# A planner that weaves convolutions into a stream of absolute differences: TensorE's rates, its slack and the place of ScalarE's sums changed in its account

## The chip, the cores and the metric

The kernel runs on one core of a Trainium2 chip. A core has TensorE (PE) for matrix products, VectorE (DVE) and ScalarE (ACT) for element work, GpSimd (POOL), SyncE (SP) for most DMA issues, and 16 DMA engines. The metric is the device time of one execution in microseconds (us), as the median of several executions.

## The reference

The input x has 16 images of 32 channels of 128 x 128. Four layers are applied, each as x = x + f(gn(x)), with gn a normalisation over groups of two channels:

```python
x = x + _L0_conv_ref(_gn(x), ...)   # skewed rows through an LSTM-like recurrence over the width
x = x + _L1_conv_ref(_gn(x), ...)   # AdderNet: out = -sum |patch - w| over 32 channels x 9 taps, on quantised values
x = x + _L2_conv_ref(_gn(x), ...)   # 2-d Hartley transform, mix 32 x 32 modes, transform back
x = x + _L3_conv_ref(_gn(x), ...)   # five edge operators, each normalised; conv, pool, conv, pool, conv, pool,
                                    # conv, and three (deconv, conv) pairs; times the input
```

Layer 1 is the long one here: for each of 32 output channels, 288 values of |patch - w| are summed at every place of every image. No matrix product does this. The kernel makes max(patch - w, 0) for whole tiles on DVE or ACT and lets TensorE add them up over the channels.

## The kernel before, in words

**Stage 0** (to about 685 us of the trace) does the first layer. The change doesn't touch it.

**The differences** (class `Differences`, method `run`, L682 on) do the second layer in 32 halves: 16 images with two halves of 64 rows each. A half has 72 steps (8 groups of four output channels by 9 taps). Each step makes one difference tile of 128 partitions by 64 rows by 128 columns, on DVE (L760, three buffers) or on ACT (L757, two buffers), whichever would end first by the account. For each difference TensorE issues a *sum*: 16 products (L647) into four PSUM banks. Nine *linear* taps a half (L662) add the part of |a - b| that is linear in a. At the end of a half DVE takes the result out of PSUM (`finish`, L628) and stores it. Four images form a group, and when a group's images are done, the third and fourth layers can run for it.

**The background** (class `After`) does the third and fourth layer for groups 0, 1 and 2 beside the differences, and for group 3 after them. It is a Python generator. Each `yield us` hands over the TensorE time of the products just issued; `yield -us` asks for a pause; `yield SUMMED` asks to wait until TensorE is done by the account. Its parts, in order, for each group:

- forward transform (L1110, L1125, L1082), mixing of modes in 32 ky steps (L1221), whose weights come in eight loads of 1024 KB through three buffers
- inverse transform: 32 steps into `o1` (L1295), then 16 steps back to full size with the residual (L1345)
- Gram products for the statistics of the edge operators (L1487), 128 steps
- the folded operators and conv1: side columns in 22 steps (L1837), then eight chunks of 16 rows with 25 taps each (L1863), each chunk followed by edge additions (L1898), pooling (L1757) and ACT's spread into `y1` (L1771)
- conv2 to conv4 (L1661), the composed upsampling layers (L908, L934), and the last one, in four units of two rounds with two sets of four taps, which DVE multiplies into the residual (L2024)

**The planner** (class `Weave`) decides while the program is written in which order each engine gets its instructions; nothing is decided on the chip. It keeps three accounts, `pe`, `dve` and `act`, which say when each engine will be done. After each difference on DVE, `run` issues the sums of all differences that have ended by DVE's account (local function `sums`), and charges PE_US for each. Then `advance(due)` runs background steps as long as TensorE could start one early enough before `due`, the time at which the next sum will be asked for:

```python
            start = max(self.pe, self.ready)
            if start + 1.0 > due + SLACK:
                return
            us = self.step()
            if us:
                self.pe = start + us * CLOCK
```

If TensorE is still early after that, `keep_busy` issues products with zeros (L677). Evictions that follow `SUMMED` are put into DVE's order at `lag()` after the present, which is the account's lateness of TensorE plus 1.0. `keep_order` then fixes each engine's order as it was written, so an instruction that waits holds up everything behind it on its engine.

**The drain** (`drain`): once the differences are written, what is left of group 2 and all of group 3 are written alternately, the one whose own clock is earlier first; `SUMMED` is then a fixed 4.5, pauses are stretched by 1.5 while both live, and mixing makes no pauses.

Of the kernel before, what the change touches and what calls it, by code (L numbers as in the profile page):

```python
# [485 lines left out]

DVE_US, ACT_US, PE_US = 2.36, 7.15, 1.0
LATE = 1.5
SLACK, CLOCK = 3.0, 1.0
SUMMED = ("summed",)  # L490
# [29 lines left out]
class Differences:  # L520
# [134 lines left out]
    def linear(self, acc, q, tap):  # L655

        kh, kw = tap // 3, tap % 3
        for j in range(4):
            for k in range(4):
                rows = slice(32 * k, 32 * k + 32)  # L660
                row = 16 * j + 4 * k + kh
                self.nc.tensor.matmul(  # L662
                    acc[k][32 * j : 32 * j + 32, :],
                    self.sel16[rows, 8, :],
                    q[rows, row : row + 4, kw : kw + W],
                    start=False,
                    stop=False,
                )
        self.weave.pe = max(self.weave.pe, self.weave.now) + 0.45

    def keep_busy(self, acc, q, until):


        start = max(self.weave.pe, self.weave.now)
        for k in range(min(int((until - start - 0.1) / 0.25), 4)):
            for j in range(4):
                self.nc.tensor.matmul(  # L677
                    acc[k][32 * j : 32 * j + 32, :], self.zero, q[:, :4, :W], start=False, stop=False
                )
            self.weave.pe = start + 0.25 * (k + 1)  # L680

    def run(self, tc, ctx, weave):  # L682
# [29 lines left out]
        for b in range(B):  # L712
            for half in range(2):
                q, xq = following, xq if half else {}
                unit = {"b": b, "half": half, "acc": None, "late": [], "summed": 0}
                for i in range(72):
# [36 lines left out]
                    dst = t if kw == 1 else t[:, :, :W]  # L753
                    unit["late"].append((ends[act], i, act, t))
                    count[act] += 1
# [77 lines left out]
class Composed:  # L833
# [60 lines left out]
    def round(self, src, n, acc, pick, quarter=0):  # L894
# [5 lines left out]
        nc, t = self.nc, self.t  # L900
        for tap in range(4):
            for j in range(4):
                for blk in range(4):
# [11 lines left out]
                    )  # L915
            yield rows * n / 512 * 0.2 + 0.95
            if tap != 2:
# [45 lines left out]
class After:  # L963
# [76 lines left out]
    def forward(self, g):  # L1040
# [4 lines left out]
        with self.pool("t_m") as mp:  # L1045
# [6 lines left out]
            with self.pool("t_t") as tp, ExitStack() as rows:  # L1052
# [24 lines left out]
                def second(n):  # L1077
# [21 lines left out]
                    steps[n] = outs[n] = weave.summed(out)  # L1099
                    return 1.45  # L1100

# [4 lines left out]
                def first(n):  # L1106
# [10 lines left out]
                    ready[n, 0] = weave.summed(out)  # L1117
                    return 1.05

                def turned(n):  # L1120

                    weave.done(ready[n, 0])
                    p = self.acc()
                    for a in range(4):
                        nc.tensor.transpose(p[:, 128 * a : 128 * a + 128], ta[n][:, a, :], cst["ident128"])  # L1125
                    ready[n, 1] = weave.summed(lambda: scaled(n, p))
                    return 1.5

# [82 lines left out]
    def mixing(self, g, xs, wp, wt):  # L1211
# [5 lines left out]
        for ky in range(M1):  # L1217
# [10 lines left out]
            if ky % 4 == 3 and len(wt) < M1 // 4:  # L1228
                wt.append(self.weights(wp, len(wt)))
            yield 1.0  # L1230
            if ky % 4 == 3 and 8 < ky < M1 - 1 and not weave.draining:
                yield -2.5
        yield SUMMED
# [14 lines left out]
    def back(self, g, load):  # L1248
# [6 lines left out]
        with self.pool("t_z") as zp_, self.pool("t_r", ahead) as rp:  # L1255
# [33 lines left out]
            for oh in range(2):  # L1289
                pa = [self.acc() for _ in range(4)]  # L1290
                for o in range(16):
                    for r in range(4):
                        for blk in range(4):
# [7 lines left out]
                            )  # L1301
                    yield 1.1
                yield SUMMED
# [35 lines left out]
            for n in range(16):  # L1339
                s, half = n // 2, n % 2  # L1340
                pf = [self.acc() for _ in range(2)]
                for i in range(4):
                    for r in range(2):
# [7 lines left out]
                        )  # L1351
                yield 0.8
                if previous:
# [103 lines left out]
    def statistics(self, g, pool, frames, sides, out, tables):  # L1457
# [38 lines left out]
        for ch in range(H // 16):  # L1496
# [3 lines left out]
            for l in range(2, 18):  # L1500
# [10 lines left out]
                if first < last:  # L1511
                    products(xp, l, slice(l + first, l + last), 64, 68 * first, False, r == H - 3)
                yield 0.5
                if l not in (9, 17):
# [122 lines left out]
    def small_layers(self, cp, rp, y1, y2):  # L1637
# [11 lines left out]
        def conv(src, n, name, evict):  # L1649
            rows = min(n // 4, 512 // n)  # L1650
            for r in range(0, n, 4 * rows):
# [3 lines left out]
                for tap in range(9):  # L1655
                    kh, kw = tap // 3, tap % 3
                    for j in range(4):
                        for blk in range(4):
# [8 lines left out]
                            )  # L1667
                    yield rows * n / 512 * 1.0 + 0.15
                yield SUMMED
# [137 lines left out]
    def conv1(self, g, pool, frames, y1, sides, wf, b1):  # L1807
# [19 lines left out]
        for s, n in enumerate("lr"):  # L1827
            for tap in range(11):
                for j in range(4):
                    for blk in range(4):  # L1830
# [13 lines left out]
                        )  # L1844
                yield 0.6
        yield SUMMED
# [6 lines left out]
        for ch in range(H // R):  # L1853
# [4 lines left out]
            for tap in range(25):  # L1858
# [11 lines left out]
                if edge and tap == 23:  # L1870
                    n, j, first, row = edge
                    for part, col, wide in ((n, 0, 5), (n + "l", 1, 2), (n + "r", W + 1, 2)):
                        width = W if wide == 5 else 1
                        o = first + (W - 1 if part == n + "r" else 0)
                        for cut_tap in range(2 * wide + 1):
                            for blk in range(4):
# [10 lines left out]
                                )  # L1887
                            yield 0.3
                yield 1.15
            yield SUMMED  # L1890
# [312 lines left out]
```

## Time and profile before

| | us |
|---|---|
| device time, median of 3 runs (6602.0 to 6603.86) | 6603.08 |
| the profiled execution's own device time | 6607.96 |
| its span, first to last instruction | 6606.2 |
| busy in it: PE, DVE, ACT | 5331.0, 5543.3, 5422.6 |
| differences on DVE (L760): 1678, mean | 2.360 |
| differences on ACT (L757): 626, mean | 7.148 |
| products with zeros (L677): 5676, busy | 407.2 |
| granted TensorE clock, mean | 0.919 |

A busy TensorE isn't one at its peak: its products are pipelined and their ends are modelled, so starts are the better measure. Four products of a sum run beside each other on four column tiles, and the 16 of a conv1 tap on 16 tiles of the array, so the mean time of one product isn't its cost. A float32 product shows as two records. Idle time is given with what ended it.

### The profile page before, as it was taken

The numbers are of one execution on the slowest core, as the hardware profiler recorded it, in microseconds if no ns is written. First come the engines' busy times: TensorE is split into PE (matmuls) and PEld (weight loads), VectorE is DVE, ScalarE is ACT, GpSimd is POOL, SyncE is SP. The second block draws the span as 40 slices with busy tenths as digits, with TensorE's granted clock in tenths as the row PEclk, the third lists the DMA queues.
The fourth block names the chain that finished last, engine by engine and source line by source line (L and its number), as shares of the span: only waits on it lengthen the run. The fifth ranks groups of instructions, "written<-read, shape, count | busy, mean of one in ns | idle before, by whom it ended". The sixth has DMA issues, their size and how long they took to land.

```text
span 6606.2 us, 269623 instructions
## 1 busy us (share of the span) xinstructions
PE 5331.0 (81%) x126486; PEld 2789.1 (42%) x126486; DVE 5543.3 (84%) x6844; ACT 5422.6 (82%) x3179; POOL 70.0 (1%) x67
## 2 busy tenths in 40 slices
PE   3798677788777879997887769998877779888796
PEld 3676233333334433333333433333333433445584
DVE  7898899999999989998899999999999999233322
ACT  3898899999999999998999989999999999112112
POOL 0000000000000000000000000000000000000000
PEclk9999899999998989998999889999999889987798
DMA  7553322221253632211553642121553641422302
GB/s 315 216 188 116 78 57 62 54 54 46 59 155 107 200 96 59 70 45 42 121 154 91 210 133 61 49 63 37 124 151 89 194 137 34 155 76 73 85 4 64
DMA packets 360800, 681.08 MB, mean 103 GB/s; under 512 B 71236, under 2 KB 219716, under 8 KB 348804
## 3 DMA queue, kind: packets, MB, share of 16 engines
q1 hardware_dynamic: 352212, 629.41, 33.3%
q0 software_dynamic: 7040, 33.80, 1.5%
q8 instruction: 989, 16.20, 1.0%
q14 instruction: 127, 1.04, 0.1%
q10 hardware_dynamic: 432, 0.64, 0.0%
HBM read 481.00 MB, written 182.69 MB: 100 GB/s over the span
## 4 chain that ended last, share of the span: by engine, by line
issue 33%; PE 29%; DVE 18%; ACT 15%; DMA 4%; SPq 1%; POOL 0%; DVEq 0%; ACTq 0%; POOLq 0%
PE acc L1863 11%; DVE d_dve L760 11%; ACT d_act L757 10%; PE acc L647 8%; PE pg L223 3%; PE acc L908 2%; PE acc L1661 2%; ACT gt L237 2%; DVE y L1768 1%; ACT junk L198 1%; DVE stat L124 1%; DMA xm_d<-xm 1%; DMA x_in<-in_x_dram 1%; DVE pooled L1757 1%; DMA v<-fold_d 1%
## 5 line engine op out<-in xcount | busy, mean ns | idle before, releaser
L757 ACT ACTIVATE d_act<-q,neg 128x8192 f16<-128x8192 f16 (+1 forms) x626 | 4428.1, 7148 | 159.2 <-PE acc L647 132.3
L760 DVE TENSOR_SCALAR d_dve<-q,qw 128x8192 f16<-128x8192 f16 (+1 forms) x1678 | 3871.1, 2360 | 174.4 <-PE acc L647 154.6
L647 PE MATMUL acc<-d_dve,sel 128*32 128x512 f16 x26848 | 1871.4, 401 | 445.5 <-DVE d_dve L760 346.8
L647 PEld LDWEIGHTS <-sel 128*32 128x32 f16 x36864 | 1003.6, 100 | 2088.2 <-issue 1416.4
L647 PE MATMUL acc<-d_act,sel 128*32 128x512 f16 x10016 | 728.0, 412 | 313.8 <-ACT d_act L757 299.3
L1863 PE MATMUL acc<-xp,wf 32*32 32x512 f32 x19200 | 757.3, 614 | 16.1 <-issue 12.9
L1771 ACT ACTIVATE y<-pooled,b 32x128 f32<-32x128 f32 x456 | 182.4, 400 | 429.9 <-DVE pooled L1757 423.7
L677 PE MATMUL acc<-q,zero 128*32 128x512 f16 x5676 | 407.2, 398 | 0.5 <-issue 0.5
L1863 PEld LDWEIGHTS acc<-xp,wf 32*32 32x32 f32 x19200 | 257.1, 104 | 324.9 <-issue 277.3
L223 PE MATMUL pg<-h,wb 64*64 64x20 f32 (+15 forms) x8192 | 345.9, 308 | 54.4 <-DVE h L251 29.5
L908 PE MATMUL acc<-y,u_conv 32*32 32x256 f32 (+1 forms) x9984 | 332.9, 447 | 68.0 <-issue 50.1
L237 ACT ACTIVATE gt<-pg,bias 128x20 f32<-128x20 f32 (+15 forms) x1024 | 332.7, 385 | 40.2 <-PE pg L223 37.8
L223 PEld LDWEIGHTS pg<-h,wb 64*64 64x64 f32 x8192 | 255.3, 153 | 129.9 <-DVE h L251 77.0
L677 PEld LDWEIGHTS <-zero 128*32 128x32 f16 x5676 | 169.6, 101 | 156.4 <-issue 31.5
L908 PEld LDWEIGHTS acc<-y,u_conv 32*32 32x32 f32 x9984 | 154.4, 109 | 190.7 <-issue 142.3
L1898 DVE TENSOR_TENSOR acc<-acc,cut 128x4 f32<-128x4 f32 x256 | 36.0, 164 | 227.8 <-PE acc L1863 225.3
L1863 PE MATMUL acc<-image,wf 32*32 32x512 f32 x6400 | 218.7, 599 | 0.6 <-issue 0.4
L223 PE MATMUL pg<-xn,wb 64*64 64x2 f32 (+63 forms) x4096 | 186.9, 293 | 25.5 <-issue 17.2
L1661 PE MATMUL acc<-y,w_conv 32*32 32x512 f32 (+2 forms) x4608 | 172.2, 528 | 37.0 <-issue 18.5
L1487 PE MATMUL acc<-xp 32*64 32x204 f32 (+2 forms) x6432 | 180.1, 337 | 26.1 <-issue 26.0
L1994 ACT ACTIVATE xr<-xr,l_ms 128x1024 f32<-128x1024 f32 x48 | 51.6, 1147 | 164.8 <-DVE xr L2024 110.8
L1863 PEld LDWEIGHTS acc<-image,wf 32*32 32x32 f32 x6400 | 169.7, 103 | 37.9 <-issue 8.7
(247 smaller groups left out, 3994.5 us busy)
## 6 DMA issues: line engine op xcount, KB each, us to landing
q<-q_d SPq DMA_DIRECT2D x128, 536.2 KB, 9.9
x_in<-in_x_dram SPq DMA_DIRECT2D x16, 2048.0 KB, 14.7
xn<-in_xs_dram SPq DMA_DIRECT2D x64, 512.0 KB, 7.1
res<-in_x_dram SPq DMA_DIRECT2D x64, 512.0 KB, 8.9
x_d<-res SPq DMA_DIRECT2D x64, 512.0 KB, 5.0
xq<-x_d SPq DMA_DIRECT2D x256, 128.0 KB, 4.1
xr<-x_d SPq DMA_DIRECT2D x256, 128.0 KB, 4.9
x_d<-xr SPq DMA_DIRECT2D x256, 128.0 KB, 2.6
```

The lines of the kernel that those rows point to most:

```text
L124: nc.vector.bn_stats(stat0[:, g, 8 * q + k, :], t[:, k * 512 : (k + 1) * 512])
L223: nc.tensor.matmul(bank[c][q][64 * pair : 64 * pair + 64, :, :width], wb[half, 4 * kind + KIND[q]].rearrange("p b o -> p (b o)"), v[half], ...
L237: nc.scalar.activation(gt[:, q, :, :n], bank[c][q][:, :, :n], AF.Tanh if q == G else AF.Sigmoid, bias=bias[:, KIND[q] : KIND[q] + 1],)
L647: self.nc.tensor.matmul(acc[k][32 * j : 32 * j + 32, :], self.sel16[:, i // 9, :], d[:, row : row + 4, c : c + W], start=first, stop=last,)
L677: self.nc.tensor.matmul(acc[k][32 * j : 32 * j + 32, :], self.zero, q[:, :4, :W], start=False, stop=False)
L757: nc.scalar.activation(dst, src, AF.Relu, bias=self.neg[:, i : i + 1])
L760: nc.vector.tensor_scalar(dst, src, self.qw[:, i : i + 1], 0.0, ALU.subtract, ALU.max)
L908: nc.tensor.matmul(acc[blk][32 * j : 32 * j + 32, o : o + rows * n], t[part, 4 * par + tap, :], own[:, top : top + rows, left : left + n], ...
L1487: nc.tensor.matmul(gram[blk][j : j + width, at : at + n], xp[part, l, 2 + j : 2 + j + width], xp[part, rows, j : j + width + 4], start=sta ...
L1661: nc.tensor.matmul(acc[blk][32 * j : 32 * j + 32, : rows * n], wc[name][part, tap, :], src[part, at : at + rows, kw : kw + n], start=tap == 0,
L1771: nc.scalar.activation(d, s, AF.Identity, bias=bj)
L1863: nc.tensor.matmul(acc[blk][32 * j : 32 * j + 32, :], tap_of("all", tap)[rows], xp[rows, 4 * j + kh : 4 * j + kh + 4, kw : kw + W], start= ...
```

## The change

Only constants of the account and one term change; the same instructions with the same operands are issued, apart from the number of products with zeros. What changes is the order in which each engine gets them, and so on TensorE which sums stand before which background steps, and on DVE and ACT which evictions stand before which differences.

- PE_US, the charge for a sum: 1.0 to 0.88. The charge for a linear tap: 0.45 to 0.36. For four products with zeros: 0.25 to 0.22.
- SLACK, how far beyond `due` a background step may still be written: 3.0 to 1.0. As `advance` adds 1.0 to the start, a step may now start no later than `due`; before, up to 2.0 later.
- ACT_SPARE: the sum of an ACT difference is placed as if it ended 1.5 us later. The choice between DVE and ACT and the account of ACT don't see this.
- The background's charges: conv1 tap 1.15 to 1.06, its edge taps 0.3 to 0.1; a tap of the upsampling layers from 0.2 x + 0.95 to 0.78 x + 0.28 and one of conv2 to conv4 from 1.0 x + 0.15 to 0.78 x + 0.28, with x the columns over 512; mixing 1.0 to 0.3, its pauses 2.5 to 5.5; inverse transform 1.1 to 0.35 and 0.8 to 0.4; Gram step 0.5 to 0.38; side columns 0.6 to 0.35; forward transform 1.05, 1.5 and 1.45 to 0.9, 1.0 and 1.2.

```diff
-DVE_US, ACT_US, PE_US = 2.36, 7.15, 1.0
-LATE = 1.5
-SLACK, CLOCK = 3.0, 1.0
+DVE_US, ACT_US, PE_US = 2.36, 7.15, 0.88
+LATE, ACT_SPARE = 1.5, 1.5
+SLACK, CLOCK = 1.0, 1.0
...
-        self.weave.pe = max(self.weave.pe, self.weave.now) + 0.45
+        self.weave.pe = max(self.weave.pe, self.weave.now) + 0.36
...
-        for k in range(min(int((until - start - 0.1) / 0.25), 4)):
+        for k in range(min(int((until - start - 0.1) / 0.22), 4)):
...
-            self.weave.pe = start + 0.25 * (k + 1)
+            self.weave.pe = start + 0.22 * (k + 1)
...
-                    unit["late"].append((ends[act], i, act, t))
+                    unit["late"].append((ends[act] + (ACT_SPARE if act else 0.0), i, act, t))
...
-            yield rows * n / 512 * 0.2 + 0.95
+            yield rows * n / 512 * 0.78 + 0.28
...
-                    return 1.45
+                    return 1.2
...
-                    return 1.05
+                    return 0.9
...
-                    return 1.5
+                    return 1.0
...
-            yield 1.0
+            yield 0.3
             if ky % 4 == 3 and 8 < ky < M1 - 1 and not weave.draining:
-                yield -2.5
+                yield -5.5
...
-                    yield 1.1
+                    yield 0.35
...
-                yield 0.8
+                yield 0.4
...
-                yield 0.5
+                yield 0.38
...
-                    yield rows * n / 512 * 1.0 + 0.15
+                    yield rows * n / 512 * 0.78 + 0.28
...
-                yield 0.6
+                yield 0.35
...
-                            yield 0.3
-                yield 1.15
+                            yield 0.1
+                yield 1.06
```

## The prediction

> **What bounds the kernel now.** I read the page's slices first, then busy time by stage, then group 2's place in the trace, then the waits, then TensorE's order of time.
>
> ```profile
> PE   3798677788777879997887769998877779888796
> ...
> DVE  7898899999999989998899999999999999233322
> ACT  3898899999999999998999989999999999112112
> ```
>
> Each digit is a tenth of a slice of 165 us. VectorE and ScalarE are full until slice 34 and nearly idle afterwards, while TensorE works on. So there are two parts to ask about: the differences (until about 5614 us) and the drain after them.
>
> ```profile
> 685.00:1841.00 1156.00, 893.52 (x15886) 430.84 (x15889) 1135.42 (x878) 1130.21 (x177) 0.00 (x0) 0.94 0.23 57
> ...
> 2437.00:2990.00 553.00, 523.52 (x11624) 203.03 (x11629) 516.42 (x345) 540.25 (x197) 0.00 (x0) 0.98 0.23 60
> ...
> 5614.00:6199.00 585.00, 468.12 (x13846) 266.01 (x13829) 204.58 (x573) 85.64 (x175) 6.69 (x13) 0.82 0.37 103
> 6199.00:6606.00 407.00, 345.55 (x12144) 269.43 (x12137) 96.95 (x276) 72.65 (x140) 0.00 (x0) 0.94 0.14 39
> ```
>
> Columns: stretch, its length, busy PE, weight loads, DVE, ACT, POOL, granted clock, DMA share, GB/s. Before 1841 no image group is ready: DVE and ACT bound, and TensorE fills up with zero products. In conv1 of group 0 (second row) TensorE is at 95%, and DVE loses 37 us. The drain lasts 992 us, with TensorE 82% busy and DVE idle.
>
> ```profile
> L1863 PE MATMUL acc<-xp,wf x6400: 584/597/1057, 2437.4 to 2979.5; 32*32 32x512 f32 x194
> ...
> L1863 PE MATMUL acc<-xp,wf x6400: 584/597/1058, 5463.9 to 5879.3; 32*32 32x512 f32 x194
> ```
>
> conv1's products of groups 0 and 2 (first and last start at the end). 6400 records are 200 taps of 16 products with two records each. Group 2's conv1 runs over the end of the differences: 1761 records are before 5614, so 55 taps, and 145 fall into the drain. What TensorE does not finish beside the differences is paid there.
>
> ```profile
> 2619.82 1.15 PE L1863 MATMUL acc<-xp,wf 32*32 32x512 f32 x32
> 2620.89 1.05 PE L647 MATMUL acc<-d_dve,sel 128*32 128x512 f16 x16
> 2621.87 1.15 PE L1863 MATMUL acc<-xp,wf 32*32 32x512 f32 x32
> 2622.95 1.06 PE L647 MATMUL acc<-d_act,sel 128*32 128x512 f16 x16
> 2623.84 1.04 PE L647 MATMUL acc<-d_dve,sel 128*32 128x512 f16 x16
> 2624.80 1.15 PE L1863 MATMUL acc<-xp,wf 32*32 32x512 f32 x32
> ```
>
> From start to start: a tap before a sum 1.07, a sum before a tap 0.97, a sum before a sum 0.87 to 0.89. One DVE step holds 1.37 sums (1678 DVE and 626 ACT differences), so sums and one tap take 1.07 + 0.97 + 0.37 x 0.87 = 2.36 us, exactly one DVE difference (mean 2360 ns). A tap per step is all that TensorE can carry.
>
> ```profile
> PE acc L647 <- ACT d_act L757: 299.3, 185, 6.1
> ...
> DVE d_dve L760 <- PE acc L647: 154.6, 115, 8.6
> ...
> ACT d_act L757 <- PE acc L647: 132.3, 47, 19.8
> ```
>
> DVE and ACT wait 287 us for buffers that late sums free; TensorE waits 299 us for ScalarE's differences.
>
> **What the Trainium skill says.** "TensorE: Matmul & The Clock Gate", section "Wait — 56ns, not 53.3ns?": warm products of 512 columns start 216 ns apart; a sum is four such steps on four column tiles, 0.86; in the trace a sum takes 0.86 beside zero products (1379.65 to 1380.51), which agrees. "TensorEngine Tiling (Array Packing)", section "Key Properties": changing the tiling mode drains the engine. The 0.97 against 0.87 above agrees with about 0.1 per change, which the new 0.88 leaves out. The first page again, "The mechanism": products stay in order, so a sum stands behind a background product that waits; the trace's DVE waits for L647 agree. Its opening table gives VectorE a strict FIFO; no row here contradicts it: an eviction placed too early holds up all later differences.
>
> **Weights for DVE and ACT time.** A half makes 72 differences at 2.36 and 7.15 us, so with d us of other DVE work and a of ACT, (T-d)/2.36 + (T-a)/7.15 = 72. T is 128, plus 0.75 d, plus 0.25 a. The same weights apply to idle time.
>
> **Part 1: conv1 (tap 1.15 to 1.06, sum 1.0 to 0.88, linear 0.45 to 0.36, edge tap 0.3 to 0.1).** A half with conv1 lasts 148 us. By the old account 72 sums, 9 linear taps and 2.6 at the change take 78.7, leaving 69 us or 60 taps; the trace has 1956/32 = 61 taps from 2595 to 2743, so the account is what sets the rate. The new account takes 69.2, leaving 79 us or 74 taps. With the slack cut to one step, some 3 us at each chunk end (2.9 a half) are no longer hidden: about 9 us, so I take 70 (bounds 64 and 74). On the chip 70 taps cost 70 x 1.08 + 53 x 0.97 + 19 x 0.87 + 9 linear at about 0.6 (estimate from its 0.37 alone and a tiling change) = 149 us against 139 now. TensorE becomes the bound, and a half goes to about 153. Conv1 goes from 542 to some 480 (200/70 x 153, times the 1.1 by which 542 exceeds 200/61 x 148). But conv1 then covers 0.42 halves fewer, which cost about 145 us a half elsewhere: 61 lost against 48 won, 13 us a group, **+37** for three.
>
> **Part 2: the other steps' rates, per group.** The account leaves the background 0.9 to 1.1 us of each 2.36 us step, so a microsecond taken off the account is worth two in time.
> - Mixing: 32 x 0.7 = 22 us of account off, five pauses of 2.5 become 5.5. From 64 to about 50 (three steps of 2.4, then five of 5.5 + 2.4): -14. Four ky use one 1024 KB weight load, 6.2 us to landing, against 7.9 a period; if queues delay it, the products wait and the sums with them (bounds -20 and +10).
> - Inverse transform, first half (1.1 to 0.35, 32 steps): 68 us now; two runs of 13 us plus two evictions give 36: -32. Second half (0.8 to 0.4): held by DVE work, -5.
> - Statistics (0.5 to 0.38): bound by its loads, -10. Side columns (0.6 to 0.35, 22 steps): -8. Forward: -5.
> - The last layer (1.05 to 0.67, 64 taps in 235 us): -36. Its reload, 528 KB pieces 11.1 us to landing, may surface (bound +15).
> With conv1's -60 that is **-170** on about 1470 us a group (bounds -100 and -210).
>
> **Part 3: where group 2 then stands.** Group 0 (1841 to 3338) ends near 3168, but group 1 needs the half that finishes at 3238 (some 20 later now) plus the 47 us that group 0 took: it starts at 3310, 57 us earlier. It ends at 3310 + 1461 - 170 = 4601. Group 2 follows 29 us later at 4630 (4862 now); conv1 starts at 5157 and is done at 5637.
>
> **Part 4: length of the differences.** Conv1's remainder (73%) moves in: 8 x 0.73 chunks of 3.96 us DVE (four pooled at 0.66, eight edge additions at 0.164) and of 16 ACT spreads at 0.40, so 23 and 37 us; weighted 27, with part of conv2 **+32**. TensorE as bound, **+37** (Part 1). Evictions: the new account has TensorE done earlier than it is, by 10 us a half, until DVE waits. No eviction of conv1 waits before 5614 now, so nothing shows its price; bounds 0 and 4 us at each of 24 chunk ends, I take 0.8 weighted, **+15** (the rest is under cover of a busy TensorE). Slack 3.0 to 1.0 and ScalarE's sums 1.5 us later: outside conv1 from 1841 on, DVE waits 93 and ACT 88 us for L647, weighted 92; a good fifth goes, **-20** (bounds 0 and -60), since 20 us are one wait behind the Gram reduction, which nothing here moves. ScalarE's two buffers cover the 1.5 us: the sum is due within 7.15. The zero products that disappear were filler. Sum **+64**: 5614 becomes about 5678, just past group 2's conv1.
>
> **Part 5: the drain.** It loses 145 taps x 1.08 = 157 us and some conv2 from 468 busy us in 585. Group 3's own chain stays: loads, scaling, reads of z, Gram tables. In that stretch mixing took 68 and first products 68 us between group 2's taps; alone, 32 x 0.28 and a few loads, about 20, and 30. Forward -10, second half -10, statistics 126 to about 105: -125. After 6199 group 2's last layer runs on to 6253 beside conv1; about 20 of that goes. Together **-145** (bounds -70 and -180).
>
> **Sum.** +64 - 145 = -81. The profiled execution took 6607.96 us (span 6606.2), 5 above the median 6603.08; from the median, **6522 us**.
>
> **Rivals.**
> - *Slower: TensorE overbooked.* At conv1's chunk ends DVE reaches the eviction while TensorE is late, all differences wait behind it, and afterwards TensorE has no difference to sum. For it: 95% busy now, and the account leaves out tiling changes. Against it: DVE's three buffers limit the lag to about two steps. It decides once the differences grow by over 145 us, 3.4 us weighted per chunk end beyond mine. At 5 more (120 us) the time is 6642.
> - *No change.* Group 3's chain alone (DMA and waits) holds the drain, which loses only 65: 6602. For it: the granted clock is 0.82 and 20% is idle there. Against it: mixing stretched from 9 to 68 us.
> - *Larger gain.* The late sums were mostly the slack's doing: -60, evictions cost nothing, the drain loses 165: 32 + 37 - 60 - 165 = -156, 6447. For it: waits up to 8.6 us outside conv1. Against it: many stand behind bursts of the last layer that no slack of one step prevents.
> - *The account doesn't move anything*: excluded, since 60 taps by account against 61 in the trace.
>
> **Numbers.** Mine 0.53 (own range 6470 to 6575), larger gain 0.17, no change 0.10, slower 0.20. Of no change I count 0.06 within 0.2% (about what a measurement of this kernel can tell from none), 0.02 to each side. Range 6430 to 6640.
>
> **What would show it.** Right: conv1 of group 2 done near the end of the differences; 66 to 72 taps a half; zero products fewer after 1841; mixing near 50, first products near 36 us; the drain near 850. Wrong: the edge additions waiting on L1863 in the differences for over 80 us, differences beyond 5760, mixing waiting on its weights, or a drain still over 930.

## The result and the profile after

The changed kernel takes **6563.47 us** (median of 4, 6554.69 to 6569.06) against 6603.47 us for the kernel before in the same runs: a ratio of **0.9937 (95% interval 0.992 to 0.9955)**, 40 us less. The forecast was 6522 us, 81 less. The profiled execution took 6562.63 us with a span of 6560.9, so between the two profiles the gain is 45 us.

First the slices of the page of the changed kernel (a digit is a tenth of a slice, now of 164 us):

```profile
PE   3689677788887889998877799988878799976696
...
DVE  7898899999999989999999989989989899844222
ACT  3899899999999999999999899998999999801012
```

DVE and ACT are full for one slice longer than before, and the thin end is shorter. The windows of the changed kernel say how much (stretch, length, busy PE, weight loads, DVE, ACT, POOL with their instructions, granted clock, DMA share, GB/s):

```profile
685.00:5711.00 5026.00, 4272.73 (x95428) 1967.47 (x95430) 4716.78 (x4010) 4758.88 (x1269) 69.25 (x48) 0.94 0.34 93
2387.00:2876.00 489.00, 478.31 (x11014) 184.90 (x10984) 449.77 (x304) 462.54 (x177) 0.00 (x0) 0.99 0.22 58
5228.00:5711.00 483.00, 473.00 (x10946) 184.31 (x10941) 450.52 (x292) 456.17 (x171) 1.20 (x3) 0.99 0.16 43
5711.00:6175.00 464.00, 310.15 (x9915) 214.47 (x9922) 196.47 (x523) 61.24 (x100) 6.77 (x13) 0.71 0.46 126
6175.00:6561.00 386.00, 329.29 (x11440) 271.78 (x11411) 91.31 (x275) 60.85 (x124) 0.00 (x0) 0.92 0.10 30
```

The first row is all the differences. They end at 5711, 97 us later than before, and DVE is idle for 5026.00 - 4716.78 = 309 us of it and ACT for 267; in the kernel before it was 249 and 179. The second and third rows are conv1 of groups 0 and 2, with TensorE at 98%. The last two are the drain: 850 us instead of 992, and its PE work is 639 us instead of 814. So 142 us came out of the drain and 97 went back into the differences.

```profile
L1863 PE MATMUL acc<-xp,wf x6400: 584/597/1056, 5228.2 to 5716.1; 32*32 32x512 f32 x194
```

This is conv1 of group 2 in the changed kernel (first and last start). It now ends 5 us after the differences, with one tap of 200 left over instead of 145. The goal that the account serves, filling TensorE until the last difference, is reached.

The waits of the changed kernel (total us, times, longest) say what was paid:

```profile
DVE d_dve L760 <- PE acc L647: 193.8, 179, 6.6
...
ACT d_act L757 <- PE acc L647: 187.4, 106, 10.7
...
PE acc L647 <- ACT d_act L757: 143.4, 100, 5.2
```

TensorE waits for ScalarE's differences for 143 us, no longer 299. But DVE and ACT wait for late sums for 381 us instead of 287. A slack cut from three to one was expected to make sums less late, and they are later. That is what the experiments had to explain.

**How the runs are compared.** With the weights of the prediction (72 differences a half at 2.36 and 7.15 us), a stretch of differences is 32 x 127.8 = 4090 us plus weighted other work plus weighted idle time of DVE (0.75) and ACT (0.25). For the kernel before: 609 other, 232 idle, together 4931 against 4929 measured; after: 640 and 299, 5029 against 5026. *Idle* below is this weighted figure. *Left* is the number of conv1's taps of group 2 that fall into the drain.

| run | slack | charges | ScalarE's sums | ratio (95%) | differences end | drain | idle | left |
|---|---|---|---|---|---|---|---|---|
| before | 3 | old | 0 | 1 | 5614 | 992 | 232 | 145 |
| after | 1 | new | 1.5 | 0.9937 (0.992 to 0.9955) | 5711 | 850 | 299 | 1 |
| e1_rates_only | 3 | new | 0 | 1.0159 (1.0136 to 1.0181) | 6008 | 703 | 527 | 0 |
| e7_rates_spare | 3 | new | 1.5 | 1.018 (1.0161 to 1.0199) | 6005 | 702 | 524 | 0 |
| e2_slack_only | 1 | old | 0 | 1.0175 (1.0157 to 1.0192) | 5438 | 1297 | 143 | 200 |
| e3_spare_only | 3 | old | 1.5 | 0.9946 (0.9931 to 0.9961) | 5596 | 985 | 220 | 154 |
| e4_no_spare | 1 | new | 0 | 0.9943 (0.9927 to 0.9958) | 5746 | 827 | 316 | 0 |
| e5_old_small | 1 | old mixing and inverse, else new | 1.5 | 1.0029 (1.0018 to 1.004) | 5616 | 1001 | 228 | 147 |
| e6_old_conv1 | 1 | old conv1, else new | 1.5 | 0.9965 (0.9952 to 0.9979) | 5630 | 940 | 238 | 92 |
| e9_small_spare | 3 | new mixing and inverse, else old | 1.5 | 0.9946 (0.9931 to 0.9962) | 5692 | 894 | 296 | 52 |
| e8_slack_low | 0.6 | new | 1.5 | 1.0159 (1.0144 to 1.0174) | 5507 | 1206 | 184 | 200 |
| e10_slack_mid | 0.85 | new | 1.5 | 0.9935 (0.9921 to 0.995) | 5654 | 905 | 259 | 80 |
| e11_with_switches | 1.5 | sum 0.95, conv1 1.10, else new | 1.5 | 0.994 (0.9928 to 0.9953) | 5695 | 876 | 282 | 11 |
| e12_small_mid | 1 | mixing 0.45, first inverse 0.55, else new | 1.5 | **0.9873 (0.9856 to 0.9889)** | 5633 | 881 | 231 | 55 |

Ends, drains and idle times are of one profiled execution each; ratios are against the kernel before on the same chip.

### The profile page after: what moved, and what is told of

It reads as the page before. It is cut to its first block, busy times and chain, and to the rows that moved or that the text cites. A ratio compares the mean times of both kernels' runs of the same rounds, so it can differ in the third digit from the quotient of the medians.

```text
span 6560.9 us, 274731 instructions
## 1 busy us (share of the span) xinstructions
PE 5377.1 (82%) x129066; PEld 2829.2 (43%) x129066; DVE 5566.4 (85%) x6857; ACT 5395.1 (82%) x3166; POOL 78.4 (1%) x67
## 5 line engine op out<-in xcount | busy, mean ns | idle before, releaser
L647 PE MATMUL acc<-d_dve,sel 128*32 128x512 f16 x26928 | 1872.5, 397 | 423.2 <-DVE d_dve L760 301.3
L647 PEld LDWEIGHTS <-sel 128*32 128x32 f16 x36864 | 989.2, 99 | 1966.0 <-issue 1298.4
L647 PE MATMUL acc<-d_act,sel 128*32 128x512 f16 x9936 | 707.5, 405 | 158.2 <-ACT d_act L757 143.4
L1863 PE MATMUL acc<-xp,wf 32*32 32x512 f32 x19200 | 730.4, 605 | 10.1 <-issue 9.5
L677 PE MATMUL acc<-q,zero 128*32 128x512 f16 x8256 | 566.1, 390 | 6.6 <-issue 6.6
L1863 PEld LDWEIGHTS acc<-xp,wf 32*32 32x32 f32 x19200 | 227.2, 103 | 323.5 <-issue 286.9
L677 PEld LDWEIGHTS <-zero 128*32 128x32 f16 x8256 | 238.7, 99 | 224.7 <-issue 42.9
L1863 PE MATMUL acc<-image,wf 32*32 32x512 f32 x6400 | 207.1, 604 | 0.6 <-issue 0.6
L1898 DVE TENSOR_TENSOR acc<-acc,cut 128x4 f32<-128x4 f32 x256 | 38.4, 166 | 183.9 <-PE acc L1863 180.6
L1863 PEld LDWEIGHTS acc<-image,wf 32*32 32x32 f32 x6400 | 179.7, 103 | 25.4 <-issue 4.3
L1661 PE MATMUL acc<-y,w_conv 32*32 32x512 f32 (+2 forms) x4608 | 155.8, 492 | 37.2 <-issue 22.7
```

The costliest lines, as they stand in the source:

```text
L647: self.nc.tensor.matmul(acc[k][32 * j : 32 * j + 32, :], self.sel16[:, i // 9, :], d[:, row : row + 4, c : c + W], start=first, stop=last,)
L677: self.nc.tensor.matmul(acc[k][32 * j : 32 * j + 32, :], self.zero, q[:, :4, :W], start=False, stop=False)
L1661: nc.tensor.matmul(acc[blk][32 * j : 32 * j + 32, : rows * n], wc[name][part, tap, :], src[part, at : at + rows, kw : kw + n], start=tap == 0,
L1863: nc.tensor.matmul(acc[blk][32 * j : 32 * j + 32, :], tap_of("all", tap)[rows], xp[rows, 4 * j + kh : 4 * j + kh + 4, kw : kw + W], start= ...
```

## The experiments

### Which of the three edits gives the gain

Three theories stood against each other. The expectations call them by letters: in A the new charges send the small steps in bursts that make the sums late; in B the smaller slack leaves TensorE idle by the account and holds the background back; in C ScalarE's later sums free its buffers too late. Four kernels each have a part of the change: the charges alone, the slack alone, the place of ScalarE's sums alone, and the charges with the slack.

```diff
# e1_rates_only, against after
-LATE, ACT_SPARE = 1.5, 1.5
-SLACK, CLOCK = 1.0, 1.0
+LATE, ACT_SPARE = 1.5, 0.0
+SLACK, CLOCK = 3.0, 1.0
```

> All new rates, slack back at 3.0, ScalarE's sums not moved. Theory A (small steps: mixing at 0.3 and the first inverse products at 0.35 are written in bursts that take longer than charged, and the sums behind them come late): the waits of DVE on L647 stay near the changed kernel's 194 us or above, the differences end near 5712, total within 15 us of the changed kernel's 6563. Theory B (slack: cutting it to one step left TensorE idle by the account, 8256 zero products against 5676, and held the background back): zero products fall to below 5500, group 2's conv1 starts before 5180 (5228 in the changed kernel), the drain gets 20 to 40 us shorter than 850, DVE waits go to 220 or more; total 6530 to 6580. Theory C (ScalarE's buffers are freed later by the 1.5 us): ACT waits on L647 fall from 187 to about 140.

```diff
# e2_slack_only, against before
-SLACK, CLOCK = 3.0, 1.0
+SLACK, CLOCK = 1.0, 1.0
```

> The kernel before with slack 1.0 alone. Theory A: DVE and ACT waits on L647 fall from 155 and 132 by a third, background later by 20 us a group, total 6600 to 6630. Theory B: the background loses 40 us a group or more, group 2's conv1 starts after 5560, zero products above 8000, total 6630 to 6680. Had the slack mattered as the prediction said (a fifth of the weighted waits, 20 us) and nothing been lost, the total would be 6583.

```diff
# e3_spare_only, against before
-LATE = 1.5
+LATE, ACT_SPARE = 1.5, 1.5
...
-                    unit["late"].append((ends[act], i, act, t))
+                    unit["late"].append((ends[act] + (ACT_SPARE if act else 0.0), i, act, t))
```

> The kernel before with ScalarE's sums placed 1.5 us later and nothing else. Theory C: ACT waits on L647 rise from 132 to 180 or more and the total by 8 to 20 us. Theories A and B: TensorE's waits for ScalarE's differences fall from 299 to about 150, they were under cover, total 6595 to 6610.

```diff
# e4_no_spare, against after
-LATE, ACT_SPARE = 1.5, 1.5
+LATE, ACT_SPARE = 1.5, 0.0
```

> The changed kernel with ScalarE's sums where they were. Theory C: ACT waits on L647 fall from 187 to about 140, the differences end 10 to 15 us earlier, total 6548 to 6555. Theories A and B: ACT waits stay above 170, TensorE's waits for ScalarE go from 143 back to 250 or more, total 6558 to 6572.

Later, to have the charges with ScalarE's later sums but the old slack:

```diff
# e7_rates_spare, against after
-SLACK, CLOCK = 1.0, 1.0
+SLACK, CLOCK = 3.0, 1.0
```

> New rates and ScalarE's sums 1.5 us later, with slack 3.0: the missing corner beside new rates alone (6716) and the whole change (6563). If the slack and the rates only work together (with the new rates, slack 3.0 lets sums run late at no gain in pace: idle 527 against 316), idle is 480 to 520, groups start at 3240 and 4650 as with slack 1.0, total 6675 to 6715. If it was the place of ScalarE's sums that counted, total below 6620.

The new charges without the new slack make the kernel 1.6% slower, and the new slack without the new charges 1.75%. Together they make it 0.6% faster. The windows of the two halves of the change show the two ways to lose; first the charges alone (e1), then the slack alone (e2), over all differences:

```profile
685.00:6008.00 5323.00, 4530.57 (x101856) 2150.18 (x101855) 4785.83 (x4179) 4826.84 (x1321) 63.47 (x49) 0.93 0.34 92
```

```profile
685.00:5438.00 4753.00, 3894.76 (x82379) 1762.03 (x82378) 4589.13 (x3680) 4675.04 (x1107) 40.92 (x33) 0.93 0.32 85
```

With the charges alone, DVE is idle for 5323 - 4786 = 537 us: sums come late, and its waits for L647 rise from 154.6 to 417.4 us. The groups go no faster for it than in e4: group 2 starts at 4649 against 4652. With the slack alone, DVE is idle for only 164 us and the differences end 176 us earlier, but the background falls behind: all of conv1 of group 2 is in the drain, which takes 1297 us. The slack of three was what made up for charges above the true cost, and charges near the true cost need the smaller slack. Neither has a worth of its own that could be added up: with the old charges a slack of 1 takes 89 us of idle time off (232 to 143) and adds 305 us of drain; with the new ones (e7 to after) it takes 225 off (524 to 299) and adds 148.

ScalarE's later sums alone gain 0.54% (e3), which was not expected: the differences end 18 us earlier, with 12 us less idle time, and the drain is 7 us shorter. Beside the other two edits they can't be told from nothing: 0.9943 without (e4) and 0.9937 with them. Removing them raises ACT's waits for L647 from 187 to 212 us; they don't cause waits.

The expectations missed most of this. No theory reached the 6716 us of e1 or the 6733 us of e2, none had the gain of e3, and e4 (6578 us) and e7 (6724 us) lie just above the ranges given. Theory C fails, since ACT waits more in e4 and not less. Of B's signs for e1, group 2's conv1 did start earlier (5127) and the drain was shorter, but the zero products rose to 10128 instead of falling below 5500, and the waits for late sums cost far more than B allowed.

### Which charges make the sums late

By stage, the idle time that the change added lies in two places. From the start of a group to its conv1 (transforms, mixing, statistics) it rose from 88 to 130 us over three groups, and in conv1 from 58 to 95. Of the 37 us in conv1, 25 are group 2's, whose conv1 stands beside the differences for 483 us now and for 150 us before. The first stretch is not one where TensorE is full. Two windows of the changed kernel show it, the transforms of groups 1 and 2 up to conv1, from one view:

```profile
3258.00:3812.00 554.00, 426.27 (x10096) 228.42 (x10104) 501.20 (x518) 509.55 (x123) 21.57 (x15) 0.90 0.53 154
4670.00:5228.00 558.00, 437.70 (x10308) 234.53 (x10300) 514.47 (x520) 514.50 (x126) 23.25 (x15) 0.90 0.53 154
```

TensorE is busy for 77 and 78% here, and yet DVE loses 53 and 44 us. TensorE's order of time in the first inverse transform of group 1 shows how (start, busy us, instruction, and in brackets idle time before it):

```profile
3428.28 1.05 PE L647 MATMUL acc<-d_dve,sel 128*32 128x512 f16 x16
3429.26 0.65 PE L1295 MATMUL acc<-cw,zi 32*32 32x32 f32 x53
3435.15 1.03 PE L1295 MATMUL acc<-cw,zi 32*32 32x32 f32 x75 [5.25 <-issue]
3436.12 1.90 PE L647 MATMUL acc<-d_act,sel 128*32 128x512 f16 x16
3437.80 1.14 PE L647 MATMUL acc<-d_dve,sel 128*32 128x512 f16 x16
3438.87 0.30 PE L1295 MATMUL acc<-cw,zi 32*32 32x32 f32 x21
3443.56 0.71 PE L1295 MATMUL acc<-cw,zi 32*32 32x32 f32 x43 [4.38 <-issue]
```

and DVE in the same kernel at the same time:

```profile
3428.14 6.90 DVE L760 TENSOR_SCALAR d_dve<-q,qw 128x8192 f16<-128x8192 f16 x3
3439.00 2.35 DVE L760 TENSOR_SCALAR d_dve<-q,qw 128x8192 f16<-128x8192 f16 x1 [3.96 <-PE acc L647]
3446.15 2.39 DVE L760 TENSOR_SCALAR d_dve<-q,qw 128x8320 f16<-128x8320 f16 x1 [4.79 <-PE acc L647]
```

A step of L1295 is 32 records; 53 + 75 are four steps, charged 4 x 0.35 = 1.4 us. They stand between sums at 3428.28 and 3436.12, so they held TensorE for 6.9 us. In the middle it did nothing for 5.25 us and waited for nothing that the profile names ("issue"). All 1024 records of the 32 steps are in the trace, so the gap isn't a missing record. The sum behind it was late, DVE's three buffers filled, and DVE stood still for 3.96 and then 4.79 us.

What TensorE waited for is in the same trace. The page of the changed kernel has a DMA queue that brings instructions (packets, MB, share of the DMA engines' time; each packet has 16384 bytes):

```profile
q8 instruction: 1009, 16.53, 1.0%
```

TensorE has 129066 products and as many weight loads, 258132 records, so 256 come to a packet. Count these records in order of their start: all 21 stops of over 0.8 us inside L1295 in this trace stand at the same place in the count of 256, one packet apart or several, and end 1.2 to 1.6 us after a packet of q8 has landed. The packet of the stop that ends at 3435.15 moved from 3432.22 to 3433.58. These stops are TensorE waiting for its own next instructions. Four steps of L1295, 128 products with a weight load each, use up just one packet. In the drain, with no sum near, a stop stands after every 128 products:

```profile
5937.70 1.59 PE L1295 MATMUL acc<-cw,zi 32*32 32x32 f32 x128 [3.82 <-issue]
5941.45 1.53 PE L1295 MATMUL acc<-cw,zi 32*32 32x32 f32 x128 [2.16 <-issue]
5945.47 1.53 PE L1295 MATMUL acc<-cw,zi 32*32 32x32 f32 x128 [2.49 <-issue]
```

In the differences of the changed kernel TensorE has 92 stops by "issue" of over 0.8 us, 213 us in all; 83 of them, 182 us, stand at this place of the count. In the kernel before it is 41 with 93 us. In no run did two packets of q8 start less than 3.2 us apart. Over all 14 traces (from 685 us on) a stop of this kind has a median of 1.3 us and at most 3.0 where the DMA engines were under 30% busy in the 3 us before its packet started, and a median of 2.5 us and at most 8.8 where they were over 80% busy. Around the stop of 5.25 us they were full (the share of 1.06 near the end of the row):

```profile
3427.00:3435.20 8.20, 2.96 (x208) 2.17 (x208) 8.04 (x4) 8.20 (x2) 0.00 (x0) 0.96 1.06 238
```

Two kernels test whether bursts of small steps, or conv1's charge (theory D in the expectations), make the idle time.

```diff
# e5_old_small, against after
-            yield 0.3
+            yield 1.0
...
-                yield -5.5
+                yield -2.5
...
-                    yield 0.35
+                    yield 1.1
...
-                yield 0.4
+                yield 0.8
```

> The changed kernel with the old charges of mixing (1.0, pauses 2.5) and of the inverse transform (1.1 and 0.8). The differences last 32 x 127.8 us plus weighted other work plus weighted idle; the change raised the idle from 232 to 299. Theory A (bursts of small steps charged too low hold back the sums; 41 of the 67 lie between a group's first transform and conv1): idle falls to about 260, the groups start 30 to 45 us later each, 60 to 80 of group 2's taps go to the drain, total 6575 to 6600. Theory D (conv1 overbooked is what costs): idle stays at 290 or more, total 6600 to 6630.

```diff
# e6_old_conv1, against after
-                            yield 0.1
-                yield 1.06
+                            yield 0.3
+                yield 1.15
```

> The changed kernel with conv1's old charges (1.15 and 0.3). Theory D (conv1 at 1.06 asks for more than TensorE has; 37 of the 67 us of idle lie there): conv1 goes from about 490 back to 530 us, idle falls to about 265, about 60 to 90 of group 2's taps go to the drain, total 6575 to 6605. Theory A: idle stays at 290 or more and the total goes to 6600 to 6630, since the taps then only move.

With the old mixing and inverse charges (e5) idle is back at 228 us. Of the 71 us that went, 30 lie between a group's start and its conv1 (130 to 100), and 32 in conv1, of which less stands beside the differences. TensorE's stops for instructions in the differences fall to 48 with 106 us. But group 2 starts at 4835 instead of 4670, 147 taps are left, and the total is 0.9% above the changed kernel: the bursts cost, and what they buy is worth more. With the old conv1 charge (e6) idle in conv1 falls from 64 to 28 us in groups 0 and 1, where conv1 goes back from 486 and 498 us to 541 and 544; the differences end 81 us earlier and the drain is 90 longer. Conv1's new charge is nearly a wash (0.9965 against 0.9937, intervals that just touch). Neither theory has e5: idle fell as in A, and further, but the total of 6631 us lies where D put it. The 6587 us of e6 lie in D's range.

The converse, in the old kernel with ScalarE's later sums, has only the mixing and inverse charges new:

```diff
# e9_small_spare, against e3_spare_only
-            yield 1.0
+            yield 0.3
...
-                yield -2.5
+                yield -5.5
...
-                    yield 1.1
+                    yield 0.35
...
-                yield 0.8
+                yield 0.4
```

> The kernel before with two parts of the change alone: the new charges of mixing (0.3, pauses 5.5) and of the inverse transform (0.35, 0.4), and ScalarE's sums 1.5 us later; slack 3.0, sums at 1.0 and conv1 at 1.15 stay. If the gain of the whole change comes from these two parts (about 60 us by undoing the first, 33 by the second alone), groups start near 3300 and 4770, idle stays below 260, total 6500 to 6550: better than both kernels. If the small steps only pay together with the small slack (theory A, bursts under slack 3.0), idle goes above 300, total 6580 to 6640.

These four numbers alone raise idle from 220 to 296 us, and nearly all of it (69 to 142) between the start of a group and conv1. The differences end 96 us later and the drain is 91 shorter: no gain over e3 at all. So the bursts do cause the idle time in that stretch, with conv1's charge and the slack untouched; TensorE's stops for instructions in the differences go with it, from 49 with 124 us (e3) to 80 with 177 us. The result lies between the two cases of the expectation: idle is that of the second, nearly, and the total (6578 us) is just under it.

### Is there a better slack

```diff
# e8_slack_low, against after
-SLACK, CLOCK = 1.0, 1.0
+SLACK, CLOCK = 0.6, 1.0
```

> The whole change with slack 0.6, so that a step may start no later than 0.4 before a sum is due. If lateness of sums is still what the rest of the idle consists of, idle falls from 299 to 200 to 240 and the groups start later by 20 to 50 us each: total 6540 to 6590. If the pace falls as with the old rates at slack 1.0 (groups 200 us later), total above 6650. If idle doesn't move, it is not the slack that makes it.

```diff
# e10_slack_mid, against after
-SLACK, CLOCK = 1.0, 1.0
+SLACK, CLOCK = 0.85, 1.0
```

> The whole change with slack 0.85, between 0.6 (6713, idle 184, groups at 3521 and 5191) and 1.0 (6563, idle 299, groups at 3258 and 4670). If the pace falls steadily: groups near 3360 and 4860, idle near 255, total 6560 to 6640. If it is a step at which one conv1 tap per difference no longer fits (a tap after two sums starts 1.96 after the last difference by the account, so it needs a slack of 0.6 or more), 0.85 behaves as 1.0: groups within 30 us of 3258 and 4670, total 6545 to 6575.

At 0.6 the background loses its pace, the second case of the expectation (6713 us): 200 taps are left and the drain takes 1206 us. At 0.85 groups 1 and 2 start 61 and 124 us later than at 1.0, so the pace falls by degrees and not in one step; 57 us less of differences are paid with 55 of drain, and the ratio is that of the change. Around 1.0 the slack only moves time from one part to the other; what is to be won is idle time at the same pace.

### Charges nearer to the cost

Two kernels try that. e11 charges the sum and the conv1 tap with the changes of tiling in them and gives some slack back; e12 charges the small steps between the old and the new figure.

```diff
# e11_with_switches, against after
-DVE_US, ACT_US, PE_US = 2.36, 7.15, 0.88
+DVE_US, ACT_US, PE_US = 2.36, 7.15, 0.95
...
-SLACK, CLOCK = 1.0, 1.0
+SLACK, CLOCK = 1.5, 1.0
...
-                yield 1.06
+                yield 1.1
```

> The whole change with a sum at 0.95 and a conv1 tap at 1.10, near what the trace shows where sums and taps alternate (0.98 and 1.07 with the change of tiling in it), and slack 1.5. If charging the switches ends the overbooking: idle in conv1 falls from 95 to about 50, conv1 510 to 530 us, total 6540 to 6570. If the larger slack brings back late sums (as at 3.0: idle 524), idle above 330 and total above 6590.

```diff
# e12_small_mid, against after
-            yield 0.3
+            yield 0.45
...
-                    yield 0.35
+                    yield 0.55
```

> The whole change with mixing at 0.45 and the first inverse products at 0.55, nearer to what four such steps take between sums in the trace (1.3 to 3 us, charged 1.4). If it is the burst of four steps that holds back the sums, idle from a group's first transform to conv1 falls from 130 to about 100, the groups start 5 to 15 us later each, total 6530 to 6560. If the bursts' cost is their number and not their charge, idle stays near 130 and the later start makes the total 6565 to 6590.

e11 lowers conv1's idle time from 95 to 64 us, but conv1 takes 519 and 524 us in groups 0 and 1, and the total doesn't move (0.994; at 6571 us it is at the edge of the first range).

e12 takes **6525.14 us**, 0.9873 of the kernel before (0.9856 to 0.9889), and beats both. The expectation had 6530 to 6560. Its windows (of the fastest of its four executions) over the differences and the drain:

```profile
685.00:5633.00 4948.00, 4212.50 (x93987) 1949.41 (x93987) 4707.75 (x3986) 4743.97 (x1237) 62.95 (x48) 0.95 0.35 94
5633.00:6514.00 881.00, 692.99 (x23111) 501.43 (x23087) 294.73 (x821) 134.80 (x256) 6.77 (x13) 0.83 0.29 81
```

Against the changed kernel the differences are 78 us shorter and the drain only 31 longer. Idle is 231 us, as in the kernel before, and 40 of the 68 us that it lost lie between a group's start and conv1 (130 to 90). TensorE's order of time in e12, in the same inverse transform of group 1:

```profile
3452.92 1.02 PE L1295 MATMUL acc<-cw,zi 32*32 32x32 f32 x96
3454.24 1.06 PE L647 MATMUL acc<-d_dve,sel 128*32 128x512 f16 x16 [0.30 <-DVE d_dve L760]
3455.23 0.28 PE L1295 MATMUL acc<-cw,zi 32*32 32x32 f32 x12
3456.18 0.91 PE L1295 MATMUL acc<-cw,zi 32*32 32x32 f32 x84 [0.67 <-issue]
```

There are three steps between sums instead of four, the sum at 3454.24 waits for DVE and not DVE for it, and the gap is 0.67 us. Over the 32 steps TensorE's products stop by "issue" for 4.6 us instead of 15.4. This place alone would prove little, since the DMA engines, full in the changed kernel's first bursts, were 10% busy here:

```profile
3448.00:3456.00 8.00, 6.94 (x296) 3.79 (x285) 7.96 (x6) 8.00 (x3) 0.00 (x0) 1.00 0.10 22
```

But over all the differences, stops for instructions fall from 83 with 182 us to 64 with 126. The 32 steps as a whole take no longer: 3448.4 to 3492.7, against 3427.0 to 3471.2 in the changed kernel, 44 us both. With their weight loads they use up eight packets, and the packets in this stretch started 3.4 to 4.6 us apart in e12 and 3.5 to 8.6 in the changed kernel. So TensorE got through the steps no faster when more were put between two sums; only the sums came later. e12 changes two charges at once, and which of them gives how much wasn't tried.

## Why the prediction was right in part

- **The account sets the pace.** Right. A group takes 1417 and 1412 us in the two full cycles after, against 1526 and 1495 before, and the pace follows charges and slack in every run.
- **Part 1, conv1 at some 480 us.** Right in length: 486, 498 and 488. The rate was not: the halves that lie wholly in conv1 have 58 to 63 taps in 141 to 154 us, not 70 in 153, about 0.41 taps per us, and 200 / 0.41 is 488. The factor of 1.1 in the forecast, carried over from the kernel before, made up for the rate that was too high; that was luck. The 0.42 halves and 48 us of its last sum don't follow from its own figures, which give 0.53 halves and 62 us (542 / 148 less 480 / 153, and 542 less 480), but the difference of some 13 us does.
- **Part 2, -170 per group: too large.** Mixing 54, 47 and 59 us (50 forecast), first inverse products 38, 44 and 38 (36), statistics from 139, 138 and 135 to 125, 125 and 132 (-10): these were right. The second half of the inverse and the forward transform grew (73, 69, 82 to 83, 89, 82; and 34 to 42 became 52 to 55) where -5 each was forecast. The last layer's 36 us didn't come: 242 and 210 us after, 235 and 226 before; with the slack of three (e1) it takes 205 and 202. From start to start the gain is 109 and 83 us, one at the lower bound of 100 and the other short of it. The small steps came as forecast; the sum of 170 was too large.
- **Part 3, where group 2 stands.** Right by two errors. Group 1 wasn't held by the half finished at 3238, since the images it needs were done at 3051, and at 3093 in the changed kernel; it started at 3258 and not at 3310. Group 1 then took 92 us more than forecast (1412 against 1320), and group 2 started at 4670, not 4630. Conv1 ends 5 us after the differences, where it was forecast 41 before their end.
- **Part 4, +64.** Too small by 33. Moved work is +31 (32 forecast). Idle time is +67 (32 forecast, which was 37 + 15 - 20). In conv1 it rose by 37, the figure given for TensorE being the bound, but 25 of that only because more of group 2's conv1 stands there; the 15 for evictions did not come: the edge additions (L1898) wait 4.8 us for L1863 in all before 5714, 0.6 of it in conv1 of group 2. Outside conv1 it rose by 31 (42 up to conv1, -6 before group 0, -5 after conv1) instead of falling by 20.
- **Part 5, the drain -145.** Right in the sum: -142, of which 121 before conv1 of group 3 (125 forecast) and 21 after (20). Not in its parts: mixing of group 3 took 45 us and the first products 38, where 20 and 30 were forecast, with the stops for instructions shown above; the statistics took 97 where 105 were, and the second half 48 where 52 were.
- **The rivals.** Neither TensorE overbooked in conv1 nor a drain held by its own chain is what happened. The larger gain rested on the late sums being the slack's doing. e2 shows that they are (232 to 143), and e7 that the new charges bring more back.

**The step that failed** is the term of Part 4 that reads "Slack 3.0 to 1.0 and ScalarE's sums 1.5 us later: outside conv1 from 1841 on, DVE waits 93 and ACT 88 us for L647, weighted 92; a good fifth goes, **-20**". It took the slack's effect from the kernel before, with its charges. There the slack takes off even more (89 us, e2). But the same change sends the small steps in bursts, four of them charged at 1.4 us. One such burst took 1.29 us and the next 6.9, because TensorE had to wait for its own instructions, and Part 2 booked these charges as pace alone. e9 shows their price, 76 us of idle time in the old kernel; e1 the price of all new charges at the old slack, 295 us. What is left of both is +67. e12, which keeps the rest of the change and softens two charges, goes back to 231 us of idle time and lands at 6525 us, near the forecast of 6522, which was made for the change without that softening.

The reading of zero products was wrong too: they were to become fewer after 1841, and rose there from 1376 to 3228 (in all from 5676 to 8256). A slack of one step leaves TensorE free by the account ahead of many sums (e2 with the slack alone has 6728).

**Open:** how much of the idle time the stops for instructions make. At a slack of 1 they mostly rise and fall with it from run to run, but in e1 222 us of them stand beside 527 us of idle time, so they are not all of it. No run changed the number of TensorE's instructions or the DMA traffic beside them, so that full DMA engines delay the packets is seen and not tested. Why ScalarE's later sums alone gain 33 us (25 in the profiled executions) is not settled either. Further charges around those of e12 weren't tried.

## What to carry to other kernels

In a planner for in-order engines, the charges and the slack are one setting: a large slack makes up for charges that are too high, so correcting one without the other loses (+1.6% and +1.75% here, -0.6% together). Charge a background step at what it takes in the burst in which it will be sent, between the neighbours that it will have, and not at its rate when alone; a short charge is paid by the foreground's sum that stands behind it. Count the instructions of a burst too, and not only its products' time: here 256 of them, four small steps, were a packet that had to be brought before TensorE went on. And count a change at both ends: here nearly every setting moved 50 to 300 us between the differences and the drain, and only less idle time at the same pace was a gain.

## What was not expected of the hardware

Bursts of 32-column float32 products with weight loads of their own don't run at their own rate for long: 128 records took 1.29 us once, and then 128 took 6.9 us with 5.25 us of idle time. The limit is the supply of TensorE's own instructions, which come by DMA in packets of 16384 bytes for 256 records: TensorE went on 1.2 to 1.7 us after such a packet had landed (the 83 stops in the differences of the changed kernel), and packets never started less than 3.2 us apart. The profile calls these stops "issue" and names nothing that ends them. The 32 steps of L1295 took 44 us with four or with three steps between sums.

A change of tiling costs more one way than the other. From start to start (medians in the trace of the changed kernel, conv1 stretches and between) a sum takes 0.87 us before a sum and 0.98 before a tap; a tap takes 0.89 before a tap and 1.08 before a sum. The prediction read about 0.1 per change, from the first pair alone; the second pair gives 0.19. Its sums used 1.08, so this moved none of them.
